# Transposing the negated row maxima ahead of a projection in its own PSUM bank, instead of behind it

## The chip, the cores and the metric

The kernel runs on one core of one Trainium2 chip. The metric is the device time of one execution in microseconds; lower is better. Before the change three executions took 4183.8, 4186.36 and 4187.36 us, a median of 4186.36 us.

The engines go by their short names: PE is the matrix engine (TensorE), PEld its weight loads, DVE is VectorE, ACT is ScalarE, POOL is GpSimd, SP is SyncE, which issues DMAs. SBUF is the working memory; PSUM is the small memory, in eight banks, into which PE writes its results and from which ACT and DVE read them. All data here is fp32 unless said otherwise.

## What is computed

One transformer-like layer on a batch of 4 sequences of 2048 tokens with 512 features: a layer norm, then the sum of the input, an attention with 16 heads of 32 features, and a small mixture of experts with room for 100 tokens per expert. Cut to the attention:

```python
xn = layernorm(x)                                   # x: (4, 2048, 512)
q, k, v = split(xn @ w_qkv)                         # 16 heads, 32 features each
q, k = spectral_filter(q), spectral_filter(k)       # linear, folded into the weights
scores = einsum('bhqd,bhkd->bhqk', q, k) / sqrt(32)
attn = softmax(scores, axis=-1)                     # needs each row's maximum
out = einsum('bhqk,bhkd->bhqd', attn, v)
x = x + out @ w_out + b_out + experts(xn)
```

The change concerns the row maximum that the softmax subtracts.

## The kernel before

**Tiling.** Four heads (128 features) form a group; there are 4 batches times 4 groups, the index `k` from 0 to 15. A group's 2048 queries are worked on in four blocks `n` of 512, and for each block the 2048 keys in sixteen tiles `j` of 128. One pair `(k, n)` is called a block here, one `j` of it a half: 64 blocks, 1024 halves. Two halves make a window.

**What a half does.** For its key tile, PE computes scores of 128 keys by 512 queries for four heads into PSUM banks 0 to 3 (`scores`, line 658); ACT takes their exponentials into the tiles `even` or `odd`, two heads in one instruction; and PE multiplies the exponentials of the half before by the values (`products`, line 687), which DVE adds to `num`. Beside that, the maxima of a later block are worked out: PE computes scores again, this time 128 queries by 512 keys, into two pairs of banks among 4 to 7 (`max_matmuls`, line 504), and DVE reduces each to one column of the tile `part` (`max_reduce`, line 516). Two neighbouring banks are sometimes reduced in one instruction. A block's maxima are complete some blocks' time before they are used.

**From maxima to a shift of the scores.** When a block's `part` is full, DVE takes the maximum over key tiles and negates it (`max_negate`, line 528): the tile `neg`, 128 queries by 16. One half later PE transposes `neg` by a matmul with the identity into 16 partitions by 128 columns of a bank (`max_turn`, line 535; "the turn" below). ACT copies the result twice, into `row` (as bf16) and into `rest` (`max_store`, line 544). POOL splits `rest` into further bf16 parts and SP sends them by three DMAs into `negm` (`max_split`, line 556, called at the head of the next window). At the first half of the block that they belong to, PE adds `negm` to the score banks (`shift`, line 671).

**The agenda.** The projections of the next group are spread over the halves of the current one, one tile of 128 tokens at a time, by a list of steps with costs that is written out beforehand (`plan`, line 958). `query_key` (line 424) makes q (`s` = 0) or keys (`s` = 1), `value` (line 450) makes v. Each takes one bank, writes one quarter of its 512 columns with 16 matmuls (four heads on 32 partitions each, the head on partitions 0 to 31 first, times four parts of the contraction), and ACT copies that quarter to SBUF. The turn, when one is due, goes into the next quarter of the projection's bank (`last % TQ`).

**Order.** Every engine's instructions are kept in the order of the program (`InOrder`, line 71). In the main loop a half emits: maxima and scores, exponentials, reductions, negation, products, then the agenda's steps, and then, if no projection took the turn, a turn in a bank of its own (line 1109).

**Banks.** Banks 4 to 7 are handed out by `Oldest` (line 867): `bank()` pops the one at the front of a list and puts it at the end, and counts it in `taken`. At the start of a half `pairs` divides the four into two pairs for the maxima. If exactly one bank was taken since the last half, the second pair is the last two of the list; otherwise it is the last one and its neighbour (4 with 5, 6 with 7).

Of the kernel before, what the change touches and what calls it, by code (L numbers as in the profile page):

```python
# [32 lines left out]
TQ = QB // P  # L33
# [68 lines left out]
def attention_and_top1_experts(ctx: ExitStack, tc: tile.TileContext, a: dict, out: bass.AP):  # L102
# [12 lines left out]
    turns = itertools.cycle(range(8))  # L115

    def bank():

        return array[:, next(turns), :]
# [45 lines left out]
    def probs(odd):  # L165

        name = "odd" if odd else "even"
        return probs_pool.tile([P, 2, 2, QB], F32, tag=name, name=name, bufs=3 if odd else 5)
# [249 lines left out]
    def columns(out, lhsT, rhs, **flags):  # L418

        for h in range(HG):  # L420
            at = slice(DH * h, DH * (h + 1))
            on.tensor.matmul(out[at], lhsT=lhsT[:, at], rhs=rhs, **flags)

    def query_key(k, n, s, first, last):

        here, cols = slice(first * P, last * P), slice(n * QB + first * P, n * QB + last * P)
        whole = bank()
        pq = whole[:, here]
        for r in range(NR):
            columns(pq, wg[k, s][:, r, :], xnT[:, r, cols], start=(r == 0), stop=(r == NR - 1))  # L430
        turned = max_turn(whole, last % TQ)
        if s == 0:
            if first == 0:
                qs[k, n] = qkv.tile([P, QB], F32, tag="q", name="q", bufs=5)
            on.scalar.copy(qs[k, n][:, here], pq)
        else:
            on.scalar.copy(keys[:, P + cols.start : P + cols.stop], pq)
        max_store(turned)

    def key_steps(n):  # L440

# [8 lines left out]
    def value(k, n, first, last):  # L450
        if n == 0 and first == 0:
            vs[k] = qkv.tile([P, NT, P], F32, tag="v", name="v")
        pv = bank()
        for t in range(first, last):
            i = n * TQ + t
            for r in range(NR):
                columns(
                    pv[:, t * P : (t + 1) * P],
                    xnT[:, r, i * P : (i + 1) * P],
                    wg[k, 2][:, r, :],  # L460
                    start=(r == 0),
                    stop=(r == NR - 1),
                )
        turned = max_turn(pv, last % TQ)
        done = pv[:, first * P : last * P].rearrange("p (t d) -> p t d", d=P)
        on.scalar.copy(vs[k][:, n * TQ + first : n * TQ + last, :], done)
        max_store(turned)

    def projections(k, tiles=1, kinds=None):

# [33 lines left out]
    def max_matmuls(item, half):  # L504
        k, n, m, t, u = item
        for h in range(2):
            at = DH * (2 * u + h)
            on.tensor.matmul(
                array[:, half[h], :],
                lhsT=qs[k, n][at : at + DH, t * P : (t + 1) * P],  # L510
                rhs=keys[at : at + DH, P + m * QB : P + (m + 1) * QB],
                start=True,
                stop=True,
            )
# [13 lines left out]
    def max_negate(k, n):  # L528
        negs[k, n] = small.tile([P, HG * TQ], F32, name="neg")
        part = parts.pop((k, n)).rearrange("p h t m -> p (h t) m")  # L530
        on.vector.tensor_reduce(negs[k, n], part, AX.X, ALU.max, negate=True)
# [3 lines left out]
    def max_turn(bank, quarter):  # L535

        if not negated:
            return None
        k, n = negated.pop(0)
        pn = bank[0 : HG * TQ, quarter * P : (quarter + 1) * P]  # L540
        on.tensor.matmul(pn, lhsT=negs.pop((k, n)), rhs=ident, start=True, stop=True)
        return k, n, pn

    def max_store(turned):
        if turned is None:
            return
        k, n, pn = turned
        rest = small.tile([HG * TQ, P], F32, name="rest")
        row = small.tile([HG * TQ, 3, P], BF16, name="row", bufs=2)
        on.scalar.copy(row[:, 0, :], pn)  # L550
        on.scalar.copy(rest, pn)
        closed[k, n] = rest, row
# [3 lines left out]
    def max_split(k, n):  # L556

        rest, row = closed.pop((k, n))
        for i in (1, 2):
            on.gpsimd.tensor_tensor(rest, rest, row[:, i - 1, :], ALU.subtract)  # L560
            on.gpsimd.tensor_copy(row[:, i, :], rest)
        negms[k, n] = qkv.tile([P, QB], BF16, tag="negm", name="negm", bufs=3)
        for i in range(3):
            on.sync.dma_start(out=negms[k, n][i::DH, :], in_=row[:, i, :])
# [93 lines left out]
    def scores(k, n, j, u):  # L658

        for head in (2 * u, 2 * u + 1):  # L660
            at = slice(DH * head, DH * (head + 1))
            on.tensor.matmul(
                scored(head),
                lhsT=steps_of_keys[at, j * P : (j + 1) * P],
                rhs=qs[k, n][at, :],
                start=False,
                stop=True,
                skip_group_check=True,
            )

    def shift(k, n):
        for head in range(HG):
            at = DH * head
            on.tensor.matmul(
                scored(head),
                lhsT=ones_b[at : at + 3, :],
                rhs=negms[k, n][at : at + 3, :],
                start=True,
                stop=True,
            )  # L680
# [205 lines left out]
    turns = Oldest()  # L886
# [167 lines left out]
    def pair(first, second):  # L1054
        on.gpsimd.dma_start(out=first, in_=second, accum_op=ALU.add)

    def add_to(tile, sum_before, engine):
        for u in range(2):
            engine.tensor_tensor(tile[:, u], tile[:, u], sum_before[:, u], ALU.add)
# [6 lines left out]
    for k in range(B * NG):  # L1066
        for n in range(NQ):
            num = work.tile([P, QB], F32, tag="num", name="num")
            tiles = {}
            for w in range(NW):  # L1070
                even, odd = w * WIN, w * WIN + 1
                if window in splits:
                    max_split(*splits.pop(window))
                for step in heads[2 * window]:
                    step()
                if window in pairs:
                    pair(*pairs.pop(window))
                if window in adds:
                    add_to(*adds.pop(window))
                for j in (even, odd):  # L1080
                    tiles[j] = probs(j == odd)


                    if j == 0:
                        shift(k, n)
                    halves = turns.pairs()
                    for u in range(2):
                        mate = maxima.pop(0) if maxima else None
                        if mate:
                            mh = halves[u]  # L1090
                            max_matmuls(mate, mh)
                        scores(k, n, j, u)
                        both = array[:, 2 * u : 2 * u + 2, :]
                        on.scalar.activation(tiles[j][:, u], both, AF.Exp, scale=SCALE)
                        if mate:
                            max_reduce(mate, mh, u == 0 or not costs[2 * window + (j == odd)])
                    negated.extend(fresh)
                    if negated:
                        splits[window + 1] = negated[0]
                    fresh = [full_blocks.pop(0) for _ in range(len(full_blocks))]  # L1100
                    for filled in fresh:
                        max_negate(*filled)
                    if left:
                        products(*left)
                    left = k, n, j, tiles[j], num
                    for step in agenda[2 * window + (j == odd)]:
                        step()
                    if negated:
                        max_store(max_turn(bank(), 0))
                last = (k, n) == (B * NG - 1, NQ - 1)  # L1110
                if not last or w < NW - 2:
                    pairs[window + 1] = tiles[even], tiles[odd]
                    if 0 < w:

                        due, engine = (2, on.gpsimd) if maxima else (3, on.vector)
                        adds[window + due] = tiles[even], tiles[even - WIN], engine
                if last and w == NW - 2:
                    y = chunk("xs")
                    on.sync.dma_start(out=y, in_=o[B - 1, n])
                window += 1  # L1120
            ended[k, n] = num, tiles[NT - WIN]
# [39 lines left out]
```

## Time and profile before

The profile shows one execution of 4186.89 us; its span, from the first to the last instruction on the core, is 4185.1 us.

| | us |
|---|---|
| median of the three runs shown | 4186.36 |
| profiled execution | 4186.89 |
| its span | 4185.1 |
| DVE idle before its 128x1 reductions, waiting for PE, in all | 654.7 |
| ACT, an exponential of two heads, mean | 1.021 |
| DVE, reduction of one bank, mean | 0.684 |
| DVE, reduction of two banks in one, mean (967 of them) | 1.215 |
| PE, the turn: 128 matmul records, mean | 0.273 |
| ACT, copy into `row`, and into `rest`, mean | 0.250 and 0.249 |
| ACT, copy of a projection's quarter, mean | 0.265 |

How to read it: a row of the profile names the engine, the operation, what it writes and reads by the program's names (`part<-array` reads PSUM, as `array` is the tile that covers all eight banks), the shape, the count, and the busy time or the duration. All lines bear the number of a helper, L82, because each instruction passes through `InOrder`; so one goes by names of tiles. An fp32 matmul appears as two records. The granted PE clock was 0.998 over the span.

### The profile page before, as it was taken

Reading aid. Unit: us, or ns where it says so; the run is one execution under the profiler, and the core shown is the slowest. Engines: PE = TensorE matmul, PEld = TensorE weight load, DVE = VectorE, ACT = ScalarE, POOL = GpSimd, SP = SyncE. Lnnn points to the kernel's source line nnn. Section 1 sums busy time; section 2 is a strip of 40 time slices with the busy share of each in tenths; the row PEclk is TensorE's granted clock in tenths of the full one; section 3 lists DMA queues with packets and bytes.
Section 4 is the critical chain, followed back from the end, with each engine's and each line's share of the span. In section 5 each row is a group of like instructions: output and inputs, shape, how many; then the busy total and the mean of one; then the engine's idle time right before and its main releaser. Section 6 shows DMA issues by size and latency. Waiting matters only on the chain.

```text
span 4185.1 us, 121271 instructions
## 1 busy us (share of the span) xinstructions
PE 4141.1 (99%) x52726; PEld 1840.0 (44%) x52726; DVE 3433.3 (82%) x4948; ACT 2493.9 (60%) x3436; POOL 2976.9 (71%) x2084
## 2 busy tenths in 40 slices
PE   8999999999999999999999999999999999999998
PEld 5444444444444444444444444444444443444432
DVE  6778888977888888897888888888778888788895
ACT  3555566676655556657565556666666555556665
POOL 1578776776876777776787766767678776687873
PEclk9999999999999999999999999999999999999999
DMA  3777878987788788898778778799877986778888
GB/s 115 147 148 151 167 154 164 223 194 147 145 165 160 151 160 162 192 202 185 141 154 163 156 155 158 157 200 203 171 155 145 184 159 134 152 161 163 159 169 171
DMA packets 178990, 684.96 MB, mean 164 GB/s; under 512 B 23494, under 2 KB 53352, under 8 KB 113176
## 3 DMA queue, kind: packets, MB, share of 16 engines
q0 software_dynamic: 110432, 605.83, 74.2%
q1 hardware_dynamic: 67952, 71.34, 5.2%
q8 instruction: 413, 6.77, 0.6%
q14 instruction: 121, 0.99, 0.1%
q10 hardware_dynamic: 72, 0.03, 0.0%
HBM read 71.07 MB, written 87.91 MB: 38 GB/s over the span
## 4 chain that ended last, share of the span: by engine, by line
PE 93%; DVE 4%; DMA 1%; issue 1%; ACT 1%; POOL 0%; SPq 0%; ACTq 0%; POOLq 0%; DVEq 0%
PE array L82 93%; DVE part L82 3%; DVE num L82 1%; DMA even<-odd 0%; ACT odd L82 0%; DVE factor L82 0%; DMA odd<-in_L_attn_w_qkv_dram 0%; DMA w<-in_L_attn_w_qkv_dram 0%; ACT even L82 0%; DVE even L82 0%; ACT keys L82 0%; ACT xs L82 0%; POOL ot L82 0%; SPq L82 0%; DVE stats L82 0%
## 5 line engine op out<-in xcount | busy, mean ns | idle before, releaser
L82 DVE TENSOR_REDUCE part<-array 128x1 f32<-128x512 f32 (+1 forms) x3129 | 2482.2, 848 | 673.2 <-PE array L82 666.1
L82 POOL TENSOR_TENSOR even<-even 128x1024 f32<-128x1024 f32 x876 | 2120.2, 2520 | 421.9 <-DMA even<-odd 416.9
L82 PE MATMUL array<-keys,q 32*128 32x512 f32 x8192 | 2060.4, 614 | 15.7 <-DVE part L82 5.8
L82 PE MATMUL array<-q,steps_of_keys 32*128 32x512 f32 x8192 | 2029.4, 616 | 2.5 <-ACT odd L82 2.4
L82 ACT ACTIVATE odd<-array 128x1024 f32<-128x1024 f32 x1024 | 995.7, 1021 | 475.8 <-PE array L82 403.8
L82 ACT ACTIVATE even<-array 128x1024 f32<-128x1024 f32 x1024 | 994.2, 1021 | 446.3 <-PE array L82 428.4
L82 PEld LDWEIGHTS array<-keys,q 32*128 32x128 f32 x8192 | 772.2, 184 | 580.3 <-DVE part L82 351.9
L82 PEld LDWEIGHTS array<-q,steps_of_keys 32*128 32x128 f32 x8192 | 692.6, 184 | 259.8 <-issue 228.5
L82 POOL DMA_DIRECT2D even<-odd x510 | 466.8, 917 | 366.9 <-ACT odd L82 310.8
L82 DVE TENSOR_TENSOR num<-num,array 128x512 f32<-128x512 f32 x960 | 648.6, 676 | 17.9 <-PE array L82 17.5
L82 PEld LDWEIGHTS array<-xnT,w 128*32 128x32 f32 x16384 | 458.1, 110 | 257.6 <-DVE part L82 177.3
L82 PE MATMUL array<-even,v 128*32 128x512 f32 x4096 | 545.5, 605 | 0.8 <-DVE part L82 0.8
L82 PE MATMUL array<-odd,v 128*32 128x512 f32 x4096 | 545.9, 605 | 0.0
L82 PE MATMUL array<-xnT,w 128*32 128x128 f32 x16384 | 526.7, 273 | 1.2 <-DVE part L82 0.6
L82 PEld LDWEIGHTS array<-w,xnT 128*32 128x32 f32 x8192 | 229.8, 110 | 147.9 <-DVE part L82 104.3
L82 PE MATMUL array<-wo,ot 128*32 128x512 f32 x2048 | 268.9, 598 | 5.3 <-POOL ot L82 5.3
L82 DVE RECIPROCAL factor<-den 128x64 f32<-128x64 f32 x504 | 273.5, 543 | 0.0
L82 PE MATMUL array<-w,xnT 128*32 128x128 f32 x8192 | 269.4, 273 | 1.7 <-DMA w<-in_L_attn_w_qkv_dram 1.7
L82 PEld LDWEIGHTS array<-even,v 128*32 128x32 f32 x4096 | 80.5, 108 | 389.7 <-DVE part L82 380.9
L82 PEld LDWEIGHTS array<-odd,v 128*32 128x32 f32 x4096 | 80.8, 108 | 388.5 <-DVE part L82 379.9
L82 POOL DMA_DIRECT2D out_dram<-y x63 | 85.7, 1361 | 198.0 <-ACT y L82 128.0
L82 ACT COPY q<-array 128x128 f32<-128x128 f32 x256 | 67.9, 265 | 179.3 <-PE array L82 175.5
(129 smaller groups left out, 1465.6 us busy)
## 6 DMA issues: line engine op xcount, KB each, us to landing
even<-odd POOLq DMA_DIRECT2D x510, 1024.0 KB, 8.0
out_dram<-y POOLq DMA_DIRECT2D x63, 1024.0 KB, 9.8
xs<-in_L_attn_x_dram SPq DMA_DIRECT2D x96, 256.0 KB
out_dram<-in_L_attn_x_dram SPq DMA_DIRECT2D x16, 1024.0 KB
w<-wd SPq DMA_DIRECT2D x30, 256.0 KB
w<-in_L_attn_w_qkv_dram SPq DMA_DIRECT2D x16, 256.0 KB
wo<-in_L_attn_w_out_dram SPq DMA_DIRECT2D x16, 256.0 KB
negm<-row SPq DMA_DIRECT2D x192, 4.0 KB
```

The source lines that it names most:

```text
L82: done = act(*args, **kwargs)
```

## The change

The turn and the two copies of its result are moved ahead of the projection's matmuls, in both kinds of projection. The bank and the quarter stay the same. ACT's order becomes `row`, `rest`, then the projection's copy; it was the projection's copy, `row`, `rest`. For a half in which no projection takes the turn, the bank of the turn is no longer counted in `taken`.

```diff
 def query_key(k, n, s, first, last):
         whole = bank()
         pq = whole[:, here]
+        max_store(max_turn(whole, last % TQ))
         for r in range(NR):
             columns(pq, wg[k, s][:, r, :], xnT[:, r, cols], start=(r == 0), stop=(r == NR - 1))
-        turned = max_turn(whole, last % TQ)
         if s == 0:
             if first == 0:
                 qs[k, n] = qkv.tile([P, QB], F32, tag="q", name="q", bufs=5)
             on.scalar.copy(qs[k, n][:, here], pq)
         else:
             on.scalar.copy(keys[:, P + cols.start : P + cols.stop], pq)
-        max_store(turned)
...
 def value(k, n, first, last):
         pv = bank()
+        max_store(max_turn(pv, last % TQ))
         for t in range(first, last):
...
-        turned = max_turn(pv, last % TQ)
         done = pv[:, first * P : last * P].rearrange("p (t d) -> p t d", d=P)
         on.scalar.copy(vs[k][:, n * TQ + first : n * TQ + last, :], done)
-        max_store(turned)
...
                     if negated:
                         max_store(max_turn(bank(), 0))
+                        turns.taken -= 1
```

## The prediction

> **What bounds the kernel now.** I read the page first, then who waits for the turn, then the order of time around single turns.
>
> ```profile
> span 4185.1 us, 121271 instructions
> ...
> PE 4141.1 (99%) x52726; PEld 1840.0 (44%) x52726; DVE 3433.3 (82%) x4948; ACT 2493.9 (60%) x3436; POOL 2976.9 (71%) x2084
> ...
> PE 93%; DVE 4%; DMA 1%; issue 1%; ACT 1%; POOL 0%; SPq 0%; ACTq 0%; POOLq 0%; DVEq 0%
> ```
>
> PE carries 93% of the chain that ended last; POOL and the DMA queues carry next to nothing. Whatever keeps PE from streaming is paid; whatever makes POOL or a DMA earlier is not repaid. Asked for 2380 to 2450 us alone, the chain is one piece of PE work.
>
> The instructions that touch the tile `neg`, and who waited for the PE turn:
>
> ```profile
> L82 PE MATMUL array<-square,neg x128: 272/273/283, 81.7 to 4099.9; 128*16 128x128 f32 x128
> ...
> who waited for it (us, times):
>   ACT q L82: 24.8, 29
>   ACT v L82: 15.6, 18
> ...
>   ACT keys L82: 0.9, 1
> ```
>
> 128 matmul records are 64 turns (fp32 shows as two). 29 + 18 + 1 = 48 of them are waited for by the copy of a projection: those 48 stand in a half with a projection, directly behind its matmuls. Of the other 16, one stands in the prologue and 15 in halves of their own. The rows show more: the copy of q, v or keys reads other columns of the bank than the turn writes, and yet it waited for the turn. So accesses of two engines to one bank are ordered here whatever their columns.
>
> Now the timeline of such a half (columns: start, duration, engine, line, what, times, idle before and its releaser):
>
> ```profile
> 2440.37 1.94 ACT L82 ACTIVATE odd<-array 128x1024 f32<-128x1024 f32 x2 [0.91 <-PE array L82]
> ...
> 2440.99 1.06 PE L82 MATMUL array<-even,v 128*32 128x512 f32 x8
> ...
> 2441.87 1.06 PE L82 MATMUL array<-w,xnT 128*32 128x128 f32 x32
> ...
> 2442.74 0.38 PE L82 MATMUL array<-square,neg 128*16 128x128 f32 x2
> ...
> 2443.05 0.70 PE L82 MATMUL array<-keys,q 32*128 32x512 f32 x2
> ...
> 2443.16 0.27 ACT L82 COPY v<-array 128x128 f32<-128x128 f32 x1 [0.86 <-PE array L82]
> ...
> 2443.32 0.25 ACT L82 CAST row<-array 16x128 bf16<-16x128 f32 x1
> 2443.48 0.25 ACT L82 COPY rest<-array 16x128 f32<-16x128 f32 x1
> ...
> 2444.21 2.42 DVE L82 TENSOR_REDUCE part<-array 128x1 f32<-128x512 f32 x3 [0.52 <-PE array L82]
> ```
>
> PE runs products (2440.99), projection (2441.87), turn (2442.74), and the next half's maxima (2443.05) without a gap. DVE waits 0.52 us for those maxima, so PE sets the pace here. Every such half that I compared shows these distances within 0.05 us.
>
> A half with a turn and no projection:
>
> ```profile
> 1799.39 1.22 DVE L82 TENSOR_REDUCE part<-array 128x2 f32<-128x1024 f32 x1
> ...
> 1799.84 0.38 PE L82 MATMUL array<-square,neg 128*16 128x128 f32 x2
> 1800.26 0.25 ACT L82 CAST row<-array 16x128 bf16<-16x128 f32 x1
> 1800.42 0.25 ACT L82 COPY rest<-array 16x128 f32<-16x128 f32 x1
> ```
>
> Row starts 0.42 us behind the turn's start, and rest ends at 1800.67, 0.83 behind it.
>
> **The change, part by part.**
>
> *The choice of pairs, 15 halves: nothing.* In such a half two banks have been popped: the list that began as 4, 5, 6, 7 is 6, 7, 4, 5 (or the reverse) when the next pairs are chosen. Before, with two taken, the second pair is the last bank and its neighbour: 4, 5. Now one counts as taken, and the second pair is the last two of the list: 4, 5. I went through the list for all 15 halves: the two rules name the same banks in the same order. Had a pair changed between joined and separate, it would be two reductions of 0.684 against one of 1.215 us, 0.15 us of DVE, 15 times 0.15 = 2.3 us either way.
>
> *The turn, 48 halves: moved ahead of the projection.* The work is the same: one matmul, two ACT copies, no DMA moves, and no queue of SP or POOL is passed. The turn's inputs are there: `neg` is reduced (0.22 us) one half earlier, and the bank is the one that the projection's first load waits for anyway. So the turn starts where the projection did, at 2441.87.
>
> *The copies, moved ahead of the projection's copy: a new wait on PE.* Row and rest read the bank that the projection is about to write. By the order of program the sequence is now: turn writes, ACT reads twice, projection writes, and by the reading of the `neg` rows PE must wait for ACT in between. The trace of before has no instance of a projection waiting for row or rest, so I build it from rows:
>
> - Turn at 2441.87. ACT's second exponential ends at 2440.37 + 1.94 = 2442.31, and 2441.87 + 0.42 = 2442.29 is where row starts by the half without a projection: the two agree, so ACT is no later than the turn.
> - Rest ends at 2441.87 + 0.83 = 2442.70.
> - From the end of a releaser to the waiting load: the reduction at 1799.39 ends at 1800.61, and the load and matmul it held back began at 1800.66: 0.05. So the projection starts at 2442.75 instead of 2441.87.
> - From the projection's start to the next maxima without a turn between: 1811.94 to 1812.93, 0.99 us. With a cold start: products that waited began at 2440.99 and gave way at 2441.87, 0.88 for two passes that take 0.87 in a steady stream (1801.20 to 1802.07 on the maxima's rows), so 0.01 for filling; I take 0.03, a little towards the 0.11 named below. Next maxima at 2442.75 + 0.99 + 0.03 = 2443.77.
> - Before: 2443.05. Loss 0.72 us. Gross it is a wait of 0.88 and a start of 0.03; the 0.19 that the turn took in the stream (0.31 + 0.87 - 0.99) is hidden in the wait.
>
> Both ends: low 0.62, if ACT starts row 0.10 before the exponential's recorded end, as copies of ACT overlap in the rows above (0.16 apart at 0.25 each). High 0.95: a filling of 0.11 (0.70 against 0.59 us for the first matmul after a wait on the maxima's rows) and 0.20 for the releaser, as the loads' own idle rows have it. I take 0.72, because each of its terms is a distance between rows of the same kind.
>
> Queued behind the waiting projection on PE are its other matmuls and the next half's maxima and scores; for those wait DVE's reductions (idle 0.52, so no backlog to live on) and ACT's exponentials. DVE's idle becomes 0.52 + 0.72 = 1.24. Does a later half make it good? A typical half is 3.79 us, PE's own stream, also in the halves after a turn; PE has nothing to shorten. So the loss stays.
>
> Three of the 48 differ (911.9, 1928.2 and 2944.7 us): there ACT normalizes three tiles behind the copies (912.76 for 2.22 us), and PE's transposes wait for them. Row and rest are out of the way earlier, so the normalizing starts behind the projection's copy, at 912.28 + 0.72 + 0.16 = 913.16: 0.40 late instead of 0.72.
>
> Sum: 45 x 0.72 + 3 x 0.40 = 32.4 + 1.2 = 33.6 us.
>
> *What becomes earlier.* Rest ends at 2442.70 instead of 2443.73, so POOL's split may start 1.0 us sooner (it waited 72.0 us for rest in 35 halves). That is worth nothing: POOL has 0% of the chain.
>
> **A rule against the change.** The rows of `neg` show that the copy waits for a write to other columns of its bank. The Trainium skill, "PSUM — Partial Sum Buffer", section "PSUM bank collisions raise a hardware error", says the same more finely: two engines must be kept apart per bank and quadrant of 32 partitions, and different columns do not help. By it only the head on partitions 0 to 31 collides with row and rest; but the projection issues that head first and PE's matmuls go in order, so the sum is the same 33.6. If columns alone decided, which no row here supports, it would be near 0.
>
> **The rivals.**
> - *Partly made good.* Some later wait that is not on PE's chain (DVE 4%, DMA 1%) swallows half of the delay: + 17, 4203 us. For it: 12% of halves, by DVE's idle time before their first reduction, start it with no idle. Against: those follow PE too, a half earlier.
> - *Dearer.* The two copies and the restart do not overlap, 1.2 us each: 48 x 1.2 = 58, 4244 us. Against: the half without projection shows them overlapped.
> - *No wait (the change does not do what I read).* Projection and copies are ordered by columns; then only order within ACT changes: 4186 us, within 0.2%. Against: the 48 waits above.
> - *Faster.* The place is the stretch between products and projection. If the projection is held less than the 0.19 us that the turn takes now, the turn drops out of PE's stream: at most 48 x 0.19 = 9 us, 4177. It decides when rest ends before 2442.0, but ACT's exponentials end only at 2442.31.
>
> **How the numbers follow.** The profiled execution took 4186.89 us (span 4185.1 and 1.8 around it); the median is 4186.36, 0.5 lower. From the median: 4186.4 + 33.6 = 4220. Its own ends are 48 x 0.62 = 30 (4216) and 48 x 0.95 = 46 (4232). Chances: this 0.80, partly made good 0.08, dearer 0.05, no wait 0.04, faster 0.03. The range reaches down into the partly made good case: 4207 to 4232. What can be told from no change here is 0.2%, 8 us: faster 0.03, same 0.04, slower 0.93.
>
> **What would show it.** In the changed profile: loads of the projections waiting for ACT rest, 48 times, near 0.7 us each; in a half with a turn, turn, gap of about 0.5, projection, next maxima; DVE's idle behind it near 1.2; the half without a projection unchanged, the joined reductions still 967. I am wrong if the projection's loads don't wait for ACT, if halves further on become shorter than before, or if the joined count moves.

## The result, and the profile after

The changed kernel takes 4219.06 us (median of six runs, 4216.6 to 4220.61), the kernel before, beside it, 4185.51 us (4183.7 to 4187.36): a ratio of 1.0078, 95% interval 1.0068 to 1.0088, or 33.6 us more. The profiled execution took 4219.22 us with a span of 4217.4 us, 32.3 us above that of before, at a granted clock of 0.997.

The page of the changed kernel, engines' busy time and the chain that ended last:

```profile
span 4217.4 us, 121250 instructions
...
PE 4149.6 (98%) x52726; PEld 1826.7 (43%) x52726; DVE 3435.6 (81%) x4948; ACT 2500.8 (59%) x3436; POOL 2977.5 (71%) x2084
...
PE 91%; DVE 4%; ACT 3%; DMA 1%; issue 1%; SPq 0%; ACTq 0%; POOL 0%; POOLq 0%; DVEq 0%
```

No engine has more instructions than before, PE's and ACT's busy times moved by less than 10 us. What changed is who stands on the chain: ACT had 1%, now it has 3%, and PE went from 93% to 91%.

The instructions that touch `rest`, and who waited for them, in the changed kernel:

```profile
  ACT rest L82: 48.3, 25
who waited for it (us, times):
  POOL rest L82: 48.3, 25
  PEld array L82: 37.6, 48
  PE array L82: 24.1, 48
```

The two PE rows are new. 48 loads waited 37.6 us for ACT's copy into `rest`, 0.78 us each: one for each half that has a turn and a projection. In the trace's records each of these 48 loads carries a wait for ACT's semaphore (a counter by which engines wait for each other), number 107: the order is one that the program holds. Neither idle sum is the loss itself, since each begins when the row before it ended; the loss is taken from the lengths of halves below. The copies of q, v and keys no longer stand among those that wait for the turn, which they did 48 times before.

One such half in order of time (columns as before):

```profile
2524.11 1.94 ACT L82 ACTIVATE odd<-array 128x1024 f32<-128x1024 f32 x2 [0.91 <-PE array L82]
...
2524.73 1.07 PE L82 MATMUL array<-even,v 128*32 128x512 f32 x8
...
2525.61 0.38 PE L82 MATMUL array<-square,neg 128*16 128x128 f32 x2
...
2526.03 0.26 ACT L82 CAST row<-array 16x128 bf16<-16x128 f32 x1
2526.20 0.25 ACT L82 COPY rest<-array 16x128 f32<-16x128 f32 x1
...
2526.50 0.81 PEld L82 LDWEIGHTS array<-xnT,w 128*32 128x32 f32 x32 [0.78 <-ACT rest L82]
2526.50 1.08 PE L82 MATMUL array<-xnT,w 128*32 128x128 f32 x32 [0.50 <-ACT rest L82]
...
2527.51 0.70 PE L82 MATMUL array<-keys,q 32*128 32x512 f32 x2
...
2527.65 0.27 ACT L82 COPY q<-array 128x128 f32<-128x128 f32 x1 [1.20 <-PE array L82]
...
2528.67 0.69 DVE L82 TENSOR_REDUCE part<-array 128x1 f32<-128x512 f32 x1 [1.23 <-PE array L82]
```

The turn starts where the projection used to, 0.88 us after the products. Rest ends at 2526.20 + 0.25 = 2526.45, and the projection's load and first matmul start at 2526.50. From the turn's start to the next half's maxima it is now 1.90 us; before, from the projection's start to those maxima, it was 1.18. DVE, which waited 0.52 us for them, waits 1.23.

The chain of waits (start, duration, what), first of the kernel before in 2380 to 2450 us, then of the same place in the changed kernel:

```profile
2379.94 70.11 PE array L82 x890
```

```profile
2499.95 24.09 PE array L82 x320
...
2525.03 1.02 ACT odd L82
2526.05 0.24 ACT row L82
2526.29 0.17 ACT rest L82
2526.45 0.04 issue
2526.50 33.89 PE array L82 x453
```

Where it was PE alone, it now leaves PE for an exponential, row and rest, and comes back. (The exponential ends 0.02 us behind row's start, and the turn's result arrives at the same time; which of the two row waits for is settled below, at e4.)

From one half's first exponential to the next half's, the half with the turn grew by 0.71 us (4.01 to 4.72) in 45 of the 48, and by 0.43 in the three with normalizing behind it: 45 x 0.71 + 3 x 0.43 = 33.2 us, against 32.3 between the two spans and 33.6 between the medians: the whole of the difference. In the 15 halves with a turn of their own it grew by 0.00, and all the other halves together by 1.3 us.

### The profile page after: what moved, and what is told of

Its sections match the earlier page's. It is cut to its first block, busy times and chain, and to the rows that moved or that the text cites. A ratio compares the mean times of both kernels' runs of the same rounds, so it can differ in the third digit from the quotient of the medians.

```text
span 4217.4 us, 121250 instructions
## 1 busy us (share of the span) xinstructions
PE 4149.6 (98%) x52726; PEld 1826.7 (43%) x52726; DVE 3435.6 (81%) x4948; ACT 2500.8 (59%) x3436; POOL 2977.5 (71%) x2084
## 4 chain that ended last, share of the span: by engine, by line
PE 91%; DVE 4%; ACT 3%; DMA 1%; issue 1%; SPq 0%; ACTq 0%; POOL 0%; POOLq 0%; DVEq 0%
PE array L82 91%; DVE part L82 3%; ACT odd L82 2%; DVE num L82 1%; DMA even<-odd 0%; DVE factor L82 0%; ACT row L82 0%; DMA w<-in_L_attn_w_qkv_dram 0%; DMA odd<-in_L_attn_w_qkv_dram 0%; ACT rest L82 0%; ACT even L82 0%; DMA wd<-odd 0%; DVE even L82 0%; ACT keys L82 0%; ACTq L82 0%
```

## The experiments

The wait for the two copies (theory A) has rivals: the choice of pairs, the turn's place in PE's stream, ACT's order, a fixed price of going to ACT and back. The kernel before was timed beside each group of runs; each difference is taken from the one of its own group, and the changed kernel's own is 33.6.

| run | median, us | before beside it | difference | 95% interval of the ratio |
|---|---|---|---|---|
| e1, uncounted bank alone | 4185.58 | 4186.8 | -1.2 | 0.9988 to 1.0007 |
| e2, turn first, copies last | 4185.89 | 4186.8 | -0.9 | 0.9990 to 1.0009 |
| e3, order of copies alone | 4187.4 | 4186.8 | +0.6 | 0.9992 to 1.0011 |
| e4, one copy | 4211.63 | 4186.8 | +24.8 | 1.0043 to 1.0077 |
| e5, three copies | 4234.23 | 4186.23 | +48.0 | 1.0097 to 1.0127 |
| e6, one-pass turn, order of before | 4186.13 | 4186.23 | -0.1 | 0.9991 to 1.0009 |
| e7, third copy elsewhere | 4230.74 | 4190.48 | +40.3 | 1.0072 to 1.0106 |
| e8, one-pass turn, turn first | 4199.24 | 4190.48 | +8.8 | 1.0008 to 1.0027 |

**e1: the uncounted bank alone**, against before.

```diff
                         max_store(max_turn(bank(), 0))
+                        turns.taken -= 1
```

> The kernel before with the uncounted bank alone; the projections as before. Theory A (the loss is the wait of the projection's matmuls for the two copies out of their bank; the count changes no pair): same as before, 4185.5 us, 967 joined reductions, half 11 to 12 unchanged. Rival B (the choice of pairs moves something): away from before by more than 2 us, another count of joined reductions.

No difference, and its groups of reductions show the same two counts:

```profile
L82 DVE TENSOR_REDUCE part<-array 128x1 f32<-128x512 f32 x2162 | 1383.8, 684 | 657.2 <-PE array L82 653.6
L82 DVE TENSOR_REDUCE part<-array 128x2 f32<-128x1024 f32 x967 | 1174.4, 1216 | 14.4 <-PE array L82 10.7 <-ACT even L82 2.4
```

2162 single and 967 joined, as before. This half of the change does nothing in this kernel.

**e2: the turn first, the copies last**, against the changed kernel.

```diff
-        max_store(max_turn(whole, last % TQ))
+        turned = max_turn(whole, last % TQ)
...
             on.scalar.copy(keys[:, P + cols.start : P + cols.stop], pq)
+        max_store(turned)
```

(and the same in `value`).

> The turn ahead of the projection's matmuls as in the changed kernel, but both copies behind the projection's copy on ACT as before, so nothing reads the bank between the turn and the projection. Theory A: the projection follows the turn without a gap, 4185.5 us (within 3), no load waits for ACT rest. Rival C (the place of the turn itself costs, between two streams of matmuls that use 32 columns each, by a drain of PE): 4219 us, the gap stays.

Its timeline of a half with turn and projection:

```profile
2503.84 1.06 PE L82 MATMUL array<-even,v 128*32 128x512 f32 x8
...
2504.72 0.27 PE L82 MATMUL array<-square,neg 128*16 128x128 f32 x1
...
2504.73 0.31 PE L82 MATMUL array<-xnT,w 128*32 128x128 f32 x3
2504.83 0.27 PE L82 MATMUL array<-square,neg 128*16 128x128 f32 x1
2504.86 1.12 PE L82 MATMUL array<-xnT,w 128*32 128x128 f32 x29
...
2505.90 0.70 PE L82 MATMUL array<-keys,q 32*128 32x512 f32 x2
```

Turn and projection follow each other without a gap, and 1.18 us lie between the turn's start and the next maxima, as before the change between projection and maxima. The turn's place costs nothing. No load of a projection waits for rest in this run.

**e3: the order of the copies alone**, against before: turn behind the projection, row and rest ahead of the projection's copy.

```diff
-        turned = max_turn(whole, last % TQ)
+        max_store(max_turn(whole, last % TQ))
...
             on.scalar.copy(keys[:, P + cols.start : P + cols.stop], pq)
-        max_store(turned)
```

> The turn behind the projection as before, but ACT copies row and rest ahead of the projection's quarter. Theory A: PE has nothing new to wait for, 4185.5 us (within 3); only the projection's copy is 0.3 us later. Rival D (what costs is that q, keys and v are copied later): a loss of up to 48 x 0.32 = 15 us, 4201 us.

No difference: that q, keys and v are copied later costs nothing here. Of the two moves neither costs by itself; the pair does, because together they put ACT's reads of the bank between two of PE's writes to it. (A turn in another bank than the projection's, with the copies ahead of it, was not run.)

**e4: one copy between**, against the changed kernel.

```diff
-        on.scalar.copy(row[:, 0, :], pn)
         on.scalar.copy(rest, pn)
+        on.gpsimd.tensor_copy(row[:, 0, :], rest)
```

> The changed kernel with one ACT copy out of PSUM instead of two: ACT copies rest, POOL makes row's first part from rest in SBUF. Theory A: the wait ends with the one copy, 0.16 us sooner in each of 48 halves: 4219 - 48 x 0.16 = 4211.4 us (4209 to 4214), half with turn 4.56 us instead of 4.72. Rival E (the wait is a fixed price of going from PE to ACT and back, or for the exponentials only, whatever the copies): 4219 us.

Who waited for `rest`:

```profile
  PEld array L82: 30.2, 48
  PE array L82: 16.7, 48
```

30.2 / 48 = 0.63 instead of 0.78 us for a load, 0.15 less; the half with the turn is 4.56 us. 33.6 - 24.8 = 8.8 us less in all against 7.7 expected. The wait follows the copies.

What is left of it is mostly the time until the turn's result is there for ACT, and not ACT's exponential. In the changed kernel row starts 0.42 us behind the turn's start in all 48 halves with a projection, and no sooner where ACT was already free. Here, in a half without a projection, ACT's exponential ends at 4078.05 and ACT is idle for 0.13 us:

```profile
4077.03 1.02 ACT L82 ACTIVATE odd<-array 128x1024 f32<-128x1024 f32 x1 [0.33 <-PE array L82]
...
4077.76 0.38 PE L82 MATMUL array<-square,neg 128*16 128x128 f32 x2
...
4078.18 0.26 ACT L82 CAST row<-array 16x128 bf16<-16x128 f32 x1
```

So the 0.88 us for which the projection is held are 0.42 to row's start, 0.16 to rest's start, 0.25 for rest and 0.05 to PE's load.

**e5: three copies between**, against the changed kernel.

```diff
         on.scalar.copy(rest, pn)
+        on.scalar.copy(rest, pn)
```

> The changed kernel with a third ACT copy out of the bank (rest is written twice with the same values). Theory A: the wait grows by one more copy, 0.16 us in each of 48 halves: 4219 + 7.7 = 4226.7 us (4224 to 4229), half with turn 4.88 us. Rival E (a fixed price): 4219 us.

The direction is theory A's, the size is not: 48.0 - 33.6 = 14.4 us instead of 7.7, and the half with the turn is 5.00 us, not 4.88. Its timeline says why:

```profile
2471.76 0.26 ACT L82 CAST row<-array 16x128 bf16<-16x128 f32 x1
2471.92 0.54 ACT L82 COPY rest<-array 16x128 f32<-16x128 f32 x2
```

Two copies of 0.25 us into the same place span 0.54 us: the second starts 0.28 or 0.29 behind the first, where rest follows row by 0.16. 48 x 0.28 = 13.4. In the trace's records the second of these copies carries a wait for ACT's own semaphore, 107, in all 64 turns: the program makes it wait for the first, which writes the same place. So I asked for a third copy into another place.

**e7: the third copy elsewhere**, against the changed kernel.

```diff
         on.scalar.copy(rest, pn)
+        on.scalar.copy(row[:, 1, :], pn)
```

> The changed kernel with a third ACT copy out of the bank, now into a part of row that POOL writes later, so it does not follow a copy into the same place. Theory A with copies that overlap: 0.16 us more in each of 48 halves, 4219 + 7.7 = 4226.7 us, half with turn 4.88. If instead any third copy costs 0.28 to 0.31, as with the one that wrote rest twice: 4234 us, half with turn 5.00.

Its timeline, ACT alone:

```profile
2535.91 0.26 ACT L82 CAST row<-array 16x128 bf16<-16x128 f32 x1
2536.08 0.25 ACT L82 COPY rest<-array 16x128 f32<-16x128 f32 x1
2536.24 0.25 ACT L82 CAST row<-array 16x128 bf16<-16x128 f32 x1
```

All three are 0.16 to 0.17 apart, and none of the copies into row and rest carries a wait for semaphore 107. The half with the turn is 4.87 us, and the total 40.3 - 33.6 = 6.7 us more than with two. With one, two and three copies the totals are 24.8, 33.6 and 40.3: 0.14 to 0.18 us a copy and half. The intervals of these totals overlap, so they alone would not settle it; the traces do. From the turn's start to the projection's it is 0.73, 0.88 and 1.04 us (medians of the 48 halves), and the 48 halves together grew by 25.5, 33.2 and 41.9 us. That is 0.16 us for each copy, and decides for theory A against a fixed price.

**e6: a turn of one pass**, order of before. A try at a kernel faster than both: 0.19 us of turn in 48 halves are still in PE's stream.

```diff
-        on.tensor.matmul(pn, lhsT=negs.pop((k, n)), rhs=ident, start=True, stop=True)
+        on.tensor.transpose(pn, negs.pop((k, n)), ident)
```

> The kernel before, order and all, with the turn made by PE's transpose, which leaves one record in the trace for 128 columns (the transposes of xs: 224 records for 56 tiles of four), instead of an fp32 matmul with two. Theory A's account of PE's stream: 0.19 us of turn in 48 halves shrinks by about 0.1: 4185.5 - 48 x 0.1 = 4180.7 us, half with turn 3.91 instead of 4.01. Rival (the turn's 0.19 is mostly change of shape, not columns): 4184 to 4186 us.

No gain: the expected 4180.7 us was missed, and the rival's 4184 to 4186 us is what came. In its timeline the turn is one record, but its load starts only 0.08 us before the recorded end of the projection's stream; with the fp32 matmul the turn's first load started 0.29 before that end (2442.64 against 2442.93 in the kernel before):

```profile
2442.03 1.06 PE L82 MATMUL array<-w,xnT 128*32 128x128 f32 x32
...
2443.01 0.09 PEld L82 LDWEIGHTS array<-square,neg 128*16 128x16 f32 x1 [0.20 <-issue]
2443.02 0.28 PE L82 MATMUL array<-square,neg 128*16 128x128 f32 x1
...
2443.22 0.70 PE L82 MATMUL array<-keys,q 32*128 32x512 f32 x2
```

The turn starts 0.99 us behind the projection's start, 0.12 later than the two-pass turn, and the maxima follow at 0.20: 1.19 us in all, as before.

**e8: the same turn in the place of e2.**

```diff
         pq = whole[:, here]
+        turned = max_turn(whole, last % TQ)
...
+        max_store(turned)
...
+        on.tensor.transpose(pn, negs.pop((k, n)), ident)
```

> The turn by PE's transpose, ahead of the projection, with both copies behind the projection's copy. If the 0.12 us that the one-record turn started later behind a projection belongs to that change of shape, it is gone behind products, and the half with turn becomes 3.9 instead of 4.01: 4185.5 - 48 x 0.1 = 4180.7 us. If it comes back at the other side, 4.01 and 4185.5 us.

Wrong both ways: it is slower, by 8.8 us, and the half with the turn takes 4.15 us. In its timeline there is a change on both sides of the turn:

```profile
2637.99 1.06 PE L82 MATMUL array<-even,v 128*32 128x512 f32 x8
...
2638.98 0.28 PE L82 MATMUL array<-square,neg 128*16 128x128 f32 x1
2639.19 0.81 PEld L82 LDWEIGHTS array<-xnT,w 128*32 128x32 f32 x32
2639.19 1.08 PE L82 MATMUL array<-xnT,w 128*32 128x128 f32 x32
...
2640.20 0.70 PE L82 MATMUL array<-keys,q 32*128 32x512 f32 x2
```

The turn starts 0.99 behind the products (0.88 with two passes), and the projection's first load only 0.21 behind the turn. The maxima come 2.21 us behind the products, against 2.06 with the two-pass turn in e2 (2503.84 to 2505.90): 0.15 x 48 = 7 us. Summed over the 48 halves of the trace it is 8.1 us.

No run was faster than the kernel before.

## Why the prediction was right, point by point

- **The choice of pairs, nothing.** Right, by e1: 967 joined reductions, no time.
- **A new wait of PE for the two copies, by bank.** Right. Shown by the 48 waits for rest, and by e2 and e3, where each move alone costs nothing; e4 and e7 show it follow the number of copies. That this program orders accesses to a bank whatever their columns is shown by the turn's quarter being another than the projection's in 48 of 48 waits. The rows of `neg` from which the prediction read it were a weaker ground than it says: in those 48 halves the projection's matmuls carry no count of their own, and the turn's second record carries it, so the copy had nothing earlier to wait for and its wait alone did not tell whether it needed the turn. Whether it would hold between different groups of 32 partitions of a bank, which the Trainium skill's page "PSUM — Partial Sum Buffer" (section "PSUM bank collisions raise a hardware error") excepts, was not tried: in this kernel the head on partitions 0 to 31 goes first.
- **The terms.** Right, and not only in their sum. Rest ends 0.84 behind the turn's start (0.83 predicted from the half without a projection); the load follows 0.05 later (0.05); the maxima follow the projection's start by 1.01 (0.99 + 0.03). Together 1.90 as predicted, less the 1.18 of before: 0.72 by the timeline, 0.71 by the lengths of halves.
- **The three halves with normalizing.** 0.43 measured, 0.40 predicted. The sum 33.2 against 33.6, the medians 33.6. That the medians meet the forecast to the tenth is luck: the interval of the ratio leaves 28 to 37 us.
- **The delay stays.** Right: no other half became systematically shorter (all of them together grew by 1.3 us), and DVE's idle in the half behind is 1.23 (1.24 predicted). "Partly made good" falls with that, and "dearer" with the overlap of the copies.
- **What becomes earlier is worth nothing.** Right: POOL's wait for rest fell from 72.0 us in 35 halves to 48.3 in 25, and POOL stays at 0% of the chain.
- **No wait, and faster.** Both fall with the 48 waits. The place for a gain would have been the 0.19 us of turn in PE's stream; the projection is held for 0.88 us instead. The prediction gives ACT's exponential as what forbids an earlier end of rest; at e4 the turn's own 0.42 us until row starts forbids it as well, also where ACT is free.

## What to carry to other kernels

Before an instruction is moved up, look at what its result's readers do to the bank it lands in: a small transpose that shares a PSUM bank with a large group of matmuls is cheap behind them, where its readers delay nobody, and dear ahead of them, where the writing engine must wait until the result has reached a second engine and that engine has read it. Here the way there took 0.42 us and each read 0.16 more, and an idle ACT would not have helped. In a kernel that one engine paces, a wait of 0.7 us in 48 places is found whole in the end time, and it can be built beforehand from distances between rows of the trace of before. A change to a rule of choice is worth walking through by hand: here both rules name the same banks.

## What the runs showed of the hardware

- ACT's copies of 0.25 us out of PSUM start 0.16 us apart when nothing orders them (e7), and 0.28 us apart when the second carries a wait for ACT's own semaphore, as it does when it writes where the first wrote (e5).
- ACT's copy of a turn's result starts 0.42 us behind the turn's start (two records of 0.273 us, 0.11 apart), whether ACT was at an exponential or idle (changed kernel).
- From the end of ACT's copy to the start of PE's load that waits for it: 0.05 us (changed kernel).
- A turn by PE's transpose is one record of 0.277 us instead of two of 0.273, but was not shorter in the stream: it started 0.12 us later behind a projection and 0.11 later behind products than the fp32 matmul, and in e8 the following projection's load did not begin before 0.21 us behind it (e6, e8). That its load starts later, close to the end of the running stream, is what the rows show; why is open.
